# A decoder layer with soft experts: where the softmax weights are turned, and in which order the work ahead of the first expert is issued

## The chip, the cores and the metric

One core of a Trainium2 chip. The metric is the device time of one execution in microseconds (us): the median of 12 runs is 2963.4 us, from 2962.04 to 2964.12. Everything is fp32.

Engines go by their short names: PE is TensorE (PEld its weight loads), DVE is VectorE, ACT is ScalarE, POOL is GpSimd, SP is SyncE, which here only issues DMAs. Each runs its own instructions strictly in the order in which they were written, and waits on semaphores for the others.

## The reference, cut to what matters

32 sequences of 100 tokens, 256 features; 16 heads of 16; a context of 361 rows for each sequence; 8 experts with 128 slots each and a hidden layer of 1024.

```python
def _L0_attn_ref(x, Wq, Wk, Wv, Wo):            # self-attention, causal, rotary
    score = jnp.where(causal[None], jnp.einsum('bqd,bkd->bqk', q, k), -jnp.inf)
    attn = jax.nn.softmax(score / jnp.sqrt(jnp.float32(D_K)), axis=-1)
    out = jnp.einsum('bqk,bkd->bqd', attn, v)
...
def _L0_ffn_ref(x, norm_gamma, slot_norm_gamma, slot_embeds, w1, b1, w2, b2):
    logits = jnp.einsum('bnd,esd->bnes', xn, sn)
    dispatch = jax.nn.softmax(logits, axis=1)                     # over the 100 tokens
    combine = jax.nn.softmax(logits.reshape(b, n, e * s), axis=-1)
    slots = jnp.einsum('bnd,bnes->besd', xn, dispatch)
    h = jax.nn.gelu(jnp.einsum('besd,edh->besh', slots, w1) + b1[None, :, None, :], approximate=False)
    eo = jnp.einsum('besh,ehd->besd', h, w2) + b2[None, :, None, :]
    out = jnp.einsum('bmd,bnm->bnd', eo.reshape(b, e * s, DIM), combine)
x = x + _L0_attn_ref(_layernorm(x), ...)
x = x + _L0_xattn_ref(_layernorm(x), ctx_1024, ctx_1024, ...)     # cross-attention
x = x + _L0_ffn_ref(_layernorm(x), ...)
```

## The kernel before

The 32 sequences form 8 groups of 4 (SIZES, line 16). For each group the 8 experts run one after the other on all 4 sequences at once; so there are 64 turns of an expert, each with its weights loaded anew (load_first for w1, load_second for w2 and b2, lines 1212 to 1222). While the experts of one group run, the attention of the next group is worked in between their matmuls. The first group's attention has no experts to hide behind and runs ahead of them.

An expert's turn (run_expert, from line 1456) has two halves: 32 matmul instructions of 512 columns into ph, every four followed by a gelu on ACT (line 1479), then 64 instructions of 256 columns into pe (a matmul in the code is two instructions in fp32, a transpose one). After each half of pe a small product with the combine weights (py) is added to x. Before the turn, route (line 1376) makes what the expert needs. It subtracts the maximum (dT, line 1388), takes exponentials on ACT (line 1400), sums on DVE (line 1409), a reciprocal, and a product on POOL (line 1417): that is the dispatch softmax with slots on partitions and tokens along the row. The next matmul needs tokens on partitions, so four transposes on PE turn dT into pd, and DVE copies that to disp (line 1430). Then sl, 16 matmul instructions, gathers the slots, and DVE scales them into slT (line 1446). route also makes cT, the combine weights. It begins when 4 of the 32 matmuls of the pe half are done, for the next expert.

Self-attention of one sequence (self_attention, from line 862): scores, mask and maximum on DVE (lines 770, 780), a subtraction on POOL (line 787), exponentials on ACT (line 795), sums on DVE (line 800). self_turn (line 815) then turns the probabilities with 16 transposes on PE into ps_pT, four to a PSUM bank, and ACT copies each bank to pT (line 828). self_values multiplies with the values in 32 small matmul instructions (ps_av), each on a quarter of the array.

Cross-attention does not turn its probabilities on PE after the first group. VectorE's transpose turns each 32x32 square by itself (line 1063, tile xt), and two DMAs put the squares where they belong: one writes xt to a scratch tensor xd in DRAM (line 1075), one reads it back as xpT with rows and columns of squares exchanged (line 1082). The first group (early) uses PE and ps_xpT (cross_turn, line 1098).

The order of all instructions is set when the program is built, by a planner at the head of the file. It keeps a clock of its own (pe["t"], advanced by spend, line 258) and queues of jobs for the other engines. Each job has a duration and, for DMAs, a lag after which its data count as there. run (line 222) emits a job when the clock has come to the time at which its inputs should be ready; that fixes its place in its engine's queue. Pieces of attention are generators that yield a Need (what must be ready, how many PSUM banks); drive and between step them as soon as the planner thinks the need is met. On the chip an engine waits until its data are there, whatever the lag said. SP's queue is one such order: a read that waits for its write holds back all that stands behind it.

near (line 857) says how far ahead of the running group a stream may work. drive(routing, routing) after the preparation runs the first route alone. load_constants (line 459) issues the weights' loads on ACT's queue, 17 of them.

Of the kernel before, what the change touches and what calls it, by code (L numbers as in the profile page):

```python
# [14 lines left out]
P = 128  # L15
# [8 lines left out]
def decoder_layer(ctx: ExitStack, tc: tile.TileContext, a: dict, out: bass.AP):  # L24
# [28 lines left out]
    NXP = 3  # L53
# [28 lines left out]
    idle_from = {"DVE": 0.0, "ACT": 8.0, "POOL": 6.0, "SP": 0.0}  # L82
    tables = {"now": None, "gelus": 0}

    class Buf:
# [28 lines left out]
        def written(self, by):  # L114
            self.writes.append(by)
            if self.root is not None:
                self.root.writes.append(by)
            self.used(by)

# [165 lines left out]

    rings = {
# [12 lines left out]
    class Need:  # L299
# [3 lines left out]
        def __init__(self, *reads, banks=1, pairs=0, exps=None, when=None, t=0.0):  # L303
            self.reads, self.banks, self.pairs = reads, banks, pairs
            self.exps, self.when, self.t = exps, when, t

        def time(self):
            items = [w for b in self.reads for w in b.writes]
            if self.banks:
                items += rings["small"].due(self.banks)  # L310
            if self.pairs:
                items += rings["pairs"].due(self.pairs)
            t = ends(items)
            return None if t is None else max(t + HOP, self.t)
# [4 lines left out]
    class Steps:  # L319


        def __init__(self, it):
            self.it, self.need, self.result = it, Need(banks=0), None
# [11 lines left out]
        def step(self):  # L335
            reads = self.need.reads
            try:
                self.need = next(self.it)
            except StopIteration as end:
# [4 lines left out]
    def drive(goal, *streams):  # L344


        while goal.it:
            run()
            ready = [s for s in streams if s.fits()]
            if ready:  # L350
                ready[0].step()
# [34 lines left out]
    def ring(pool_, shape, name, bufs):  # L386
# [10 lines left out]
        "p": ring(one, [S, NH, S], "p", 1), "ropeu": ring(one, [P, 4 * S], "ropeu", 1),  # L397
# [6 lines left out]
        "pT": ring(two, [S, HG * S], "pT", NQ), "ctx": ring(two, [P, len(KC), D], "ctx", 2),  # L404
# [4 lines left out]
        "xd": ring(dram, [P, 4 * NKB * HG * QB], "xd", 3),  # L409
# [8 lines left out]
        "dT": ring(wk, [P, GM, S], "dT", 2), "cT": ring(wk, [P, NTM], "cT", 3),  # L418
        "disp": ring(wk, [S, GM * NS], "disp", 1), "slT": ring(wk, [P, ND, GM * NS], "slT", 1),
# [18 lines left out]
    def load_raw(nm, at):  # L438
        raw = R["hT"].new(f"raw{nm}")
        v = raw.get().rearrange("p (c d) -> p c d", c=ND)  # L440
        nc.scalar.dma_start(out=v, in_=a[f"L0_attn_{nm}"].rearrange("(c p) d -> p c d", p=P))
        raw.written(at)
        raws[nm] = raw

# [14 lines left out]
    def load_constants():  # L459

        load_raw("Wk", 5.5)
        load_raw("Wq", 8.0)
        nc.scalar.dma_start(out=rope, in_=a["rope"].rearrange("p (m f) n -> p m f n", f=2))
        load_raw("Wv", 11.0)
        load_raw("Wo", 12.5)
        rows = Buf(ap=one.tile([P, P], F32, name="rows"))
        for r0, src in (
# [6 lines left out]
            nc.scalar.dma_start(out=rows.ap[r0 : r0 + src.shape[0], :], in_=src)  # L474
        rows.written(14.0)
        for k, nm in enumerate(("Wk", "Wq", "Wv", "Wo")):
            w = wT["x" + nm] = fixed([P, ND, D], f"xw{nm}")
            nc.scalar.dma_start(
                out=w.ap, in_=a[f"L0_xattn_{nm}"].rearrange("(c p) o -> p c o", p=P)
            )  # L480
            w.written(15.5 + 1.5 * k)
        nc.scalar.dma_start(out=bvB, in_=a["L0_xattn_bv"].partition_broadcast(P))
        nc.scalar.dma_start(out=boB, in_=a["L0_xattn_bo"].partition_broadcast(P))
        se = Buf(ap=wpool.tile([P, NE, D], F32, tag="w1", name="se"))
        nc.scalar.dma_start(out=se.ap, in_=a["L0_ffn_slot_embeds"].rearrange("e s d -> s e d"))
        se.written(26.0)
        return rows, se

    def make_constants():
# [18 lines left out]
        gps(1.5, lambda: nc.gpsimd.memset(spad.ap, 0.0), [], [spad], prio=3)  # L508
        for i in range(2):
# [10 lines left out]
    def turn_rows(rows):  # L520
        ps = bank("ps_cols")
        transpose(ps.get()[:, :NROW], rows.ap[:NROW], ident[:NROW, :NROW])
# [224 lines left out]
    def self_scores(t, kT):  # L747
# [5 lines left out]
        sc = [rings["pairs"].new("sc") for _ in range(2)]  # L753
        for c in range(ND):
            for q in range(NQ):
                rows_ = slice(q * 32, (q + 1) * 32)
                matmul(
                    sc[q // 2].get()[:S, q % 2, c * 2 * S : (c + 1) * 2 * S],
                    lhsT=qT[rows_, c, :],
                    rhs=kT.get()[rows_, c, :, :],  # L760
                    share=NQ, start=True, stop=True,
                )
        parts = []
        for i in range(2):
            hs = slice(i * HPC, (i + 1) * HPC)
# [5 lines left out]
                    p.get()[:, hs, :].rearrange("n (q h) k -> n q h k", q=2),  # L771
# [9 lines left out]
                    nmax.get()[:, hs], p.get()[:, hs, :], axis=AX.X, op=ALU.max  # L781
# [6 lines left out]
                    p.get()[:, hs, :], p.get()[:, hs, :],  # L788
# [6 lines left out]
                lambda hs=hs: nc.scalar.activation(p.get()[:, hs, :], p.get()[:, hs, :], AF.Exp),  # L795
                [part], [part], table="exp",
            )
            vec(
                0.99,
                lambda hs=hs: nc.vector.tensor_reduce(  # L800
                    sums.get()[:, hs], p.get()[:, hs, :], axis=AX.X, op=ALU.add
# [11 lines left out]
        return p, parts, widened(rinv, NH, 0.29)  # L813

    def self_turn(p, parts):

        pTs = []
        for q in range(NQ):
            yield Need(parts[q // 2])
            ps = bank("ps_pT")  # L820
            for i in range(HG):
                transpose(
                    ps.get()[:S, i * S : (i + 1) * S], p.get()[:, q * HG + i, :], ident[:S, :S]
                )
            pT = R["pT"].new()
            act(
                0.49,
                lambda pT=pT, ps=ps: nc.scalar.copy(pT.get(), ps.get()[:S, : HG * S]), [ps], [pT],
# [877 lines left out]
```

## Time and profile before

| | |
|---|---|
| median of 12 runs | 2963.4 us |
| the profiled execution | 2963.39 us, of it the span from first to last instruction 2961.6 us |
| self-attention's transposes, ps_pT | 512 instructions, mean 249 ns |
| the copies to pT on ACT (line 828) | 128, mean 494 ns |
| dispatch's transposes, pd | 256 instructions, mean 273 ns |
| the copies to disp on DVE (line 1430) | 64, mean 688 ns |
| self-attention's values, ps_av | 1024 instructions of 100 columns |
| trips through DRAM, xd and xpT | 112 each way, 768 KB each |
| loads of expert weights, w | 128 of 1024 KB |
| bytes moved by DMA | 343.58 MB, mean 116 GB/s |
| first matmul of the first expert | 220.8 us after the span's start |

A mean duration of a matmul is the time from its start to its modelled end; matmuls overlap, so it is longer than the time that one takes away from the next. An engine's busy time is the union of these. A line "A <- B: total, times, longest" is idle time of A before the instructions named, and who ended it.

### The profile page before, as it was taken

How to read it: one execution, taken by the hardware profiler on the slowest of the kernel's cores; microseconds unless marked ns; L12 is line 12 of the kernel's file. 1: busy time of each engine (PE TensorE's matmuls, PEld its weight loads, DVE VectorE, ACT ScalarE, POOL GpSimd, SP SyncE). 2: the span in 40 equal slices, each digit the busy share in tenths (PEclk: the TensorE clock that was granted, in tenths of full speed). 3: DMA queues.
4: the chain of work that ended last, by engine and by line, in shares of the span. 5: the costliest groups of instructions: out<-in, count | busy, mean ns of one | idle time of the engine just before them, and what ended most of it. 6: DMA issues, size and time to landing. Idle time of an engine off the chain costs nothing.

```text
span 2961.6 us, 42941 instructions
## 1 busy us (share of the span) xinstructions
PE 2909.6 (98%) x17393; PEld 2033.2 (69%) x17393; DVE 1368.0 (46%) x2719; ACT 1234.3 (42%) x2662; POOL 555.1 (19%) x722
## 2 busy tenths in 40 slices
PE   6989999999999999999999999999999999999999
PEld 4766766767667676677667666677676766677676
DVE  5764554546443554436444355444554345422121
ACT  3554444444443444434444444433444434433331
POOL 3413231032101221013210222002321021000000
PEclk9989999999999999999999999999999999999999
DMA  3022433335352343414443343433344234422221
GB/s 111 12 70 69 167 103 121 133 116 170 109 178 68 130 148 125 157 58 151 132 156 119 98 151 126 147 111 119 123 156 141 92 105 162 167 72 70 73 75 52
DMA packets 191574, 343.58 MB, mean 116 GB/s; under 512 B 8104, under 2 KB 160656, under 8 KB 191376
## 3 DMA queue, kind: packets, MB, share of 16 engines
q1 hardware_dynamic: 187632, 337.18, 34.0%
q10 hardware_dynamic: 3744, 3.65, 0.4%
q8 instruction: 138, 2.26, 0.3%
q14 instruction: 60, 0.49, 0.1%
HBM read 249.44 MB, written 91.36 MB: 115 GB/s over the span
## 4 chain that ended last, share of the span: by engine, by line
PE 95%; ACT 2%; DVE 1%; POOL 1%; DMA 1%; issue 0%; SPq 0%; ACTq 0%; DVEq 0%; POOLq 0%
PE pe L268 31%; PE ph L268 30%; PE sc L268 5%; PE sl L268 4%; PE py L268 4%; PE ps_lt L268 3%; PE ps_xv L268 3%; PE ps_kT L268 3%; PE ps_xav L268 2%; PE ps_qk L268 2%; PE ps_o L268 2%; PE ps_pT L272 1%; PE pd L272 1%; PE ps_v L268 1%; PE sc L272 1%; PE ps_xq L268 1%
## 5 line engine op out<-in xcount | busy, mean ns | idle before, releaser
L268 PE MATMUL pe<-w,hT 128*128 128x256 f32 x4096 | 1000.8, 383 | 0.0
L268 PE MATMUL ph<-slT,w 128*128 128x512 f32 x2048 | 964.1, 599 | 1.5 <-ACT hT L1479 1.4
L268 PEld LDWEIGHTS pe<-w,hT 128*128 128x128 f32 x4096 | 742.2, 190 | 156.4 <-issue 52.7
L1479 ACT ACTIVATE hT<-ph,cols 128x512 f32<-128x512 f32 x512 | 350.5, 687 | 799.5 <-PE ph L268 799.3
L268 PEld LDWEIGHTS ph<-slT,w 128*128 128x128 f32 x2048 | 372.0, 190 | 325.2 <-issue 290.8
L1049 ACT ACTIVATE sc<-sc,xnmax 128x361 f32<-128x361 f32 x448 | 237.6, 530 | 146.1 <-DVE xnmax L1039 138.8
L1039 DVE TENSOR_REDUCE xnmax<-sc 128x2 f32<-128x722 f32 x256 | 222.0, 903 | 165.1 <-PE sc L268 164.7
L1063 DVE STREAM_TRANSPOSE xt<-sc 128x384 f32<-128x384 f32 x448 | 231.7, 556 | 23.5 <-ACT sc L1049 18.1
L608 POOL TENSOR_SCALAR ve<-bnmv 100x1 f32<-100x1 f32 x96 | 27.7, 289 | 907.7 <-DVE bnmv L605 907.6
L1417 POOL TENSOR_TENSOR dT<-dT,ri 128x400 f32<-128x400 f32 x64 | 54.6, 853 | 721.8 <-DVE ri L1414 720.6
L1531 DVE SCALAR_TENSOR_TENSOR x<-py,cinv,x 100x256 f32<-100x256 f32 x256 | 112.7, 477 | 153.2 <-PE py L268 153.0
L1409 DVE TENSOR_REDUCE sm<-dT 128x4 f32<-128x400 f32 x64 | 34.7, 542 | 263.9 <-ACT dT L1400 263.9
L787 POOL TENSOR_TENSOR p<-p,nmax 100x800 f32<-100x800 f32 x64 | 96.5, 1523 | 315.6 <-DVE nmax L780 312.6
L1508 DVE TENSOR_TENSOR eo<-pe,b 128x512 f32<-128x512 f32 x128 | 87.6, 684 | 129.2 <-PE pe L268 128.9
L268 PEld LDWEIGHTS sl<-disp,xn 100*128 100x128 f32 x1024 | 135.7, 194 | 8.1 <-issue 1.3
L268 PE MATMUL sl<-disp,xn 100*128 100x128 f32 x1024 | 136.7, 277 | 0.9 <-DVE disp L1430 0.9
L1446 DVE TENSOR_SCALAR slT<-sl,cols 128x512 f32<-128x512 f32 x128 | 95.4, 745 | 84.3 <-PE sl L268 83.6
L268 PE MATMUL py<-eo,cT 128*100 128x256 f32 x512 | 131.5, 379 | 0.8 <-DVE eo L1508 0.8
L268 PE MATMUL sc<-kT,xqT 32*128 32x361 f32 x1024 | 125.6, 518 | 3.7 <-DVE xt L1063 2.0
L770 DVE TENSOR_TENSOR p<-sc,causal 100x800 f32<-100x800 f32 x64 | 60.4, 985 | 137.8 <-PE sc L268 137.8
L428 ACT ACT_TABLE_LOAD x93 | 119.3, 1283 | 1.5
L268 PEld LDWEIGHTS py<-eo,cT 128*100 128x100 f32 x512 | 85.4, 167 | 50.1 <-issue 29.0
(144 smaller groups left out, 3231.1 us busy)
## 6 DMA issues: line engine op xcount, KB each, us to landing
w<-in_L_ffn_w_dram SPq DMA_DIRECT2D x128, 1024.0 KB
xd<-xt SPq DMA_DIRECT2D x112, 768.0 KB
xpT<-xd SPq DMA_DIRECT2D x112, 768.0 KB
ctx<-in_ctx_dram SPq DMA_DIRECT2D x32, 256.0 KB
b<-in_L_ffn_b_dram SPq DMA_DIRECT2D x64, 128.0 KB
ctx<-in_ctx_dram SPq DMA_DIRECT2D x32, 105.0 KB
x<-in_x_dram SPq DMA_DIRECT2D x8, 400.0 KB
out_dram<-x SPq DMA_DIRECT2D x16, 200.0 KB
```

The costliest lines, as they stand in the source:

```text
L268: nc.tensor.matmul(out, lhsT=lhsT, rhs=rhs, **kw)
L272: nc.tensor.transpose(out, in_, identity)
L428: act(0.2, lambda: nc.scalar.activation(spare, mhalf[:1, :1], f), [], [], table=table, prio=2)
L770: lambda i=i, hs=hs: nc.vector.tensor_tensor(p.get()[:, hs, :].rearrange("n (q h) k -> n q h k", q=2), sc[i].get()[:S, :, : HG * S].rearra ...
L787: lambda hs=hs: nc.gpsimd.tensor_tensor(p.get()[:, hs, :], p.get()[:, hs, :], nmax.get()[:, hs].unsqueeze(2).to_broadcast([S, HPC, S]), AL ...
L1039: lambda nm=nm, sc=sc: nc.vector.tensor_reduce(nm.get(), sc.get()[:, :, :SK], axis=AX.X, op=ALU.max, negate=True),
L1049: nc.scalar.activation(to[:, :SK], sc.get()[:, i, :SK], AF.Exp, bias=nm.get()[:, i : i + 1], accum_out=sums.get()[:, c, q, r : r + 1],)
L1063: nc.vector.transpose(t_.get()[:, :, :, 2 * t + i, :].rearrange("p j c u -> p c j u"), sc.get()[:, i, : NKB * P].rearrange("p (c u j) -> p ...
L1446: lambda dc=dc, sl=sl: nc.vector.tensor_scalar(slT.get()[:, dc, : nb * NS], sl.get()[:, : nb * NS], cols.ap[:, NGM + dc : NGM + dc + 1], N ...
L1479: lambda h=h, ph_=ph_, hc=hc: nc.scalar.activation(h.get()[:, :n], ph_.get()[:, :n], AF.Gelu, bias=cols.ap[:, e * NHC + hc : e * NHC + hc ...
L1508: lambda eo=eo, po=po, m=m: nc.vector.tensor_tensor(eo.get()[:, :m], po.get().rearrange("p (i d) -> p i d", i=2)[:, :m], b2.unsqueeze(1).t ...
L1531: lambda b=b, i=i: nc.vector.scalar_tensor_tensor(xs[g].get()[:, b, :], py[:S, i, :], k.ci.get()[:, b : b + 1], xs[g].get()[:, b, :], ALU. ...
```

## The change

Four things are changed. Dispatch weights: route is split in two. soften makes dT and disp for expert e + 1 while route for expert e only uses what lies ready. For the first expert of a group soften still turns on PE; for the others DVE turns squares into dt and there_and_back sends them through DRAM to disp. Self-attention: from the fifth sequence on, squares and there_and_back take the place of self_turn, in two halves of eight heads; the tiles p and dT are padded to 128 columns, with zeros set once by POOL. Planner: the allowance of each DMA falls from 5.0 us to 4.5 (cross) or 4.0 (the new ones), that of a pair of cross-attention's squares rises from 0.95 to 1.12 us; buffers are told free when their last reader is done; streams with a lower sequence number go first; xpT has two buffers instead of three, ctx one instead of two. Ahead of the first expert: three loads stay on ACT's queue, the rest go to SP's; the self-attention scores come half by half; near lets streams work further ahead; the first route is driven together with the streams.

```diff
-    NXP = 3
+    NXP = 2
-    idle_from = {"DVE": 0.0, "ACT": 8.0, "POOL": 6.0, "SP": 0.0}
+    idle_from = {"DVE": 0.0, "ACT": 3.0, "POOL": 5.0, "SP": 0.0}
...
             if ready:
-                ready[0].step()
+                min(ready, key=lambda s: s.need.seq).step()
...
-        "p": ring(one, [S, NH, S], "p", 1), "ropeu": ring(one, [P, 4 * S], "ropeu", 1),
+        "p": Kept([const.tile([P, NH, P], F32, name="p")]), "ropeu": ring(one, [P, 4 * S], "ropeu", 1),
...
-        "pT": ring(two, [S, HG * S], "pT", NQ), "ctx": ring(two, [P, len(KC), D], "ctx", 2),
+        "st": ring(two, [P, 4, HPC, QB], "st", 1),
+        "sd": ring(dram, [P, 4 * HPC * QB], "sd", 3),
+        "pT": ring(two, [P, 4, HPC, QB], "pT", 2), "ctx": ring(two, [P, len(KC), D], "ctx", 1),
...
-        "dT": ring(wk, [P, GM, S], "dT", 2), "cT": ring(wk, [P, NTM], "cT", 3),
-        "disp": ring(wk, [S, GM * NS], "disp", 1), "slT": ring(wk, [P, ND, GM * NS], "slT", 1),
+        "dT": Kept([const.tile([P, GM, P], F32, name=f"dT{i}") for i in range(2)]),
+        "dt": ring(wk, [P, 4, GM, QB], "dt", 1), "dd": ring(dram, [P, 4 * GM * QB], "dd", 2),
+        "cT": ring(wk, [P, NTM], "cT", 3),
+        "disp": ring(wk, [P, 4, GM, QB], "disp", 2), "slT": ring(wk, [P, ND, GM * NS], "slT", 1),
...
+    def load_cross(nm, at):
+        w = wT["x" + nm] = fixed([P, ND, D], f"xw{nm}")
+        nc.sync.dma_start(out=w.ap, in_=a[f"L0_xattn_{nm}"].rearrange("(c p) o -> p c o", p=P))
+        w.written(at)
...
+        load_raw(nc.scalar, "Wk", 5.0)
+        load_raw(nc.scalar, "Wq", 6.5)
         nc.scalar.dma_start(out=rope, in_=a["rope"].rearrange("p (m f) n -> p m f n", f=2))
+        load_raw(nc.sync, "Wv", 9.0)
+        load_cross("Wk", 10.0)
...
+        zeros = gps(3.0, lambda: nc.gpsimd.memset(R["p"].tiles[0], 0.0), [], [], prio=2)
+        R["p"].first.append(zeros)
+        for i in range(2):
+            zeros = gps(1.0, lambda i=i: nc.gpsimd.memset(R["dT"].tiles[i], 0.0), [], [], prio=3)
+            R["dT"].first.append(zeros)
...
+    def squares(p, part, hs):
+
+        st, sd, pT = R["st"].new(), R["sd"].new(), R["pT"].new()
+        vec(
+            1.2,
+            lambda: nc.vector.transpose(
+                st.get().rearrange("p j h u -> p h j u"),
+                p.get()[:, hs, :].rearrange("p h (u j) -> p h j u", j=4),
+            ),
+            [part], [st],
+        )
+        there_and_back(
+            st, st.get, sd, pT, lambda: pT.get().rearrange("p g h u -> p g (h u)"), 4.0
+        )
+        return pT
+
+    def there_and_back(t, source, d, to, target, lag):
+
+
+        job(
+            "SP", 0.35,
+            lambda: nc.sync.dma_start(
+                out=d.get(), in_=source().rearrange("p j h u -> p (j h u)")
+            ),
+            [t], [d], lag=lag,
+        )
+        job(
+            "SP", 0.35,
+            lambda: nc.sync.dma_start(
+                out=target(), in_=d.get().rearrange("(g u) (j f) -> (u j) g f", u=QB, j=4)
+            ),
+            [d], [to], lag=lag,
+        )
...
+        pairs_ = ((0,), (1,)) if state["group"] < 0 else ((0, 1),)
...
+            if not early:
+                pTs.append(squares(p, part, hs))
...
+                        to = av.get()[q * 32 : (q + 1) * 32, c * n : (c + 1) * n].rearrange(
+                            "p (g u) -> p g u", u=QB
+                        )
+                        pT = pTs[q // 2].get()[:S, :, (q % 2) * HG + h, :]
...
         last = FIRST[state["group"] + 1] + SIZES[state["group"] + 1]
-        return b < last + (ahead if state["group"] >= 0 else 1)
+        return b < last + ahead
...
-                    lambda: b in queries and b in keys and state["turned"] > n - NXP
-                    and (b >= SIZES[0] or state["flipped"] > n - 2)
+                    lambda: b in queries and b in keys
+                    and (state["flipped"] > n - 2 if b < SIZES[0] else state["turned"] > n - 4)
...
-    def route(k, e):
+    def soften(k, e, first=False):
...
+        disp = R["disp"].new()
+        if first:
+            yield Need(dT)
+            pd = bank("pd")
+            for b in range(nb):
+                transpose(pd.get()[:S, b * NS : (b + 1) * NS], dT.get()[:, b, :S], ident)
...
+        else:
+            dt = R["dt"].new()
+            vec(
+                0.7,
+                lambda: nc.vector.transpose(
+                    dt.get().rearrange("p j b u -> p b j u"),
+                    dT.get().rearrange("p b (u j) -> p b j u", j=4),
+                ),
+                [dT], [dt], prio=0,
+            )
+            there_and_back(
+                dt, dt.get, R["dd"].new(), disp,
+                lambda: disp.get().rearrange("p g b u -> p g (b u)"), 4.0,
+            )
+        k.disp[e] = disp
+
+    def route(k, e):
...
+        lt, disp = k.lt[e // 2], k.disp.pop(e)
...
                 matmul(
-                    sl.get()[:, b * NS : (b + 1) * NS],
+                    sl.get()[:, b * NS : (b + 1) * NS].rearrange("p (g u) -> p g u", u=QB),
                     lhsT=k.xn.get()[:, b, dc * P : (dc + 1) * P],
-                    rhs=disp.get()[:, b * NS : (b + 1) * NS],
+                    rhs=disp.get()[:S, :, b],
...
+    def routes(k, e):
+
+        if e == 0:
+            yield from soften(k, 0, True)
+        if e + 1 < NE:
+            yield from soften(k, e + 1)
+        return (yield from route(k, e))
+
+    routing = Steps(routes(groups[0], 0))
+    ready = drive(routing, routing, *order())
```

## The prediction

> **What bounds the kernel now.** I read the page's first two parts, then the windows table, then the chain of waits inside one expert, then who waits for whom. The page says which engine has no room:
>
> ```profile
> PE 2909.6 (98%) x17393; PEld 2033.2 (69%) x17393; DVE 1368.0 (46%) x2719; ACT 1234.3 (42%) x2662; POOL 555.1 (19%) x722
> ```
>
> PE is busy 2909.6 of 2961.6 us; 52.0 us are idle, and no other engine passes half. The windows table (window, its length, busy time of PE, PEld, DVE, ACT, POOL, granted clock, DMA share, GB/s) says where they lie:
>
> ```profile
> 0.00:20.00 20.00, 5.32 (x22) 4.29 (x23) 5.67 (x8) 2.33 (x4) 6.45 (x20) 1.00 0.76 217
> ...
> 200.00:220.00 20.00, 13.57 (x66) 12.01 (x66) 9.81 (x19) 7.41 (x13) 1.88 (x2) 0.76 0.42 137
> ...
> 400.00:800.00 400.00, 399.91 (x2575) 279.47 (x2574) 204.21 (x409) 173.99 (x381) 87.85 (x111) 1.00 0.39 130
> ```
>
> From 220 us, where the first expert begins, to 2400 us PE is idle for about 1.2 us. There a microsecond off PE's queue is a microsecond off the end, and work on any other engine is free until it makes PE wait. Before 220 us PE is idle for 42.9 us (20 minus its busy time, summed over eleven windows), and the granted clock drops: busy time times (1 - clock) gives 1.1 us at 40-60, 3.1 at 60-80, 1.4 at 180-200, 3.3 at 200-220 and 1.8 at 220-240, some 10.7 us of slowed work.
>
> **TensorE work removed and added.** A matmul row's mean (250 ns for a self-attention transpose) is its pipeline depth, not its cost; the cost is the step from one start to the next, which the chain of waits shows (start, length, what):
>
> ```profile
> 1001.84 0.88 PE ph L268 x2
> 1002.73 0.34 PE ps_pT L272 x4
> 1003.07 0.88 PE ph L268 x2
> 1003.96 0.69 PE ps_pT L272 x8
> ...
> 1008.65 0.82 PE ps_av L268 x32
> ...
> 1037.28 1.18 PE ps_xav L268 x48
> ...
> 1039.08 0.44 PE pd L272 x4
> ```
>
> Self-attention's turn: 16 transposes for each of the 28 sequences after the first group are gone, 448. Four take 0.34 and eight 0.69, so 0.0865 each: 38.8 us. The first group keeps its 64.
>
> Dispatch turn: 64 experts had four transposes at 0.44 us. The first expert of each of the 8 groups keeps them (first=True), 56 lose them: 24.6 us.
>
> Added: the 32 matmuls of ps_av run over 128 instead of 100 columns for those 28 sequences. With 48 at 1.18 and 32 at 0.82 (same columns), one is 0.0225 and 0.10 fixed; times 1.28 that is 0.0288, and 32 make 1.02. So 0.20 more, 5.6 us. Both new right-hand sides are read in four strided runs. ps_xav reads such runs already and is no dearer than ps_av, which reads contiguously (24.6 against 25.6 ns), so I add nothing for sl; if that failed for its 1024 matmuls, 10% of their 136.7 us would be 14 us.
>
> Net: 38.8 + 24.6 - 5.6 = **57.8 us off PE**.
>
> The Trainium skill speaks against this: VectorE: DVE Perf Modes, Rules for kernel authors, says to turn 128x128 on TensorE where PSUM will do, and its section The three transpose paths gives 390 ns for it and calls a plain strided DMA copy 19 times slower than the hardware's own DMA transpose when the inner stride is large. By 390 ns the 672 transposes would be worth 262 us, which the steps above contradict. The strided read of xpT, already in this trace with its long inner runs, shows no such slowness; the measurement decides.
>
> **Other engines.** ACT loses 112 copies at 494 ns (55 us). DVE gains 56 squares of 1024 columns and 56 of 512, and loses 56 copies at 688 ns. No such SBUF-to-SBUF square is in the trace; the nearest is
>
> ```profile
> L1063 DVE STREAM_TRANSPOSE xt<-sc 128x384 f32<-128x384 f32 x448 | 231.7, 556 | 23.5 <-ACT sc L1049 18.1 <-DMA xd<-xt 4.9
> ```
>
> 1.45 ns a column: at most 1.48 and 0.74 us; at least, at the rate of the 1024-column reduction (1224 ns), 1.22 and 0.61. I take 1.35 and 0.7: 76 + 39 - 39 = 76 us, so DVE goes from 46 to about 50%. Its tight place is an expert's second half, 18.60 of 24 us in a window of 1020-1044; two squares there make 21.3. It still fits. If it did not, PE would wait for eo, slT or the score banks.
>
> DMA: 112 trips there and back (56 self halves of 512 KB each way, 56 dispatch of 256 KB) add 86 MB to 343.58, and the share goes from 0.39 to about 0.48. On SP a read waits for its write, and everything behind it with it; the first line is SP's longest wait for DMA, the second is from PE's own list (total, times, longest):
>
> ```profile
> SPq L1082 <- DMA xd<-xt: 332.7, 99, 8.5
> ```
>
> ```profile
> PE ps_xav L268 <- DMA xpT<-xd: 2.3, 1, 2.3
> ```
>
> 3.36 us each for 768 KB, 8.5 at worst, yet PE waited for such a trip once. SP had 112 and gets 224, up to 4 for an expert of 43 us ((2961.6 - 220.8) / 64): 4 x 3.4 = 13 us of blocking. Queued behind it are w, ctx, b and x; w has an expert's half of slack (32 ph steps of 0.43, 14 us). The dispatch trip is made one expert (31.5 us from one ph to the next in the last group, more before) ahead, so it is hidden. The self and cross trips are used as soon as the planner thinks them landed, and it now allows 4.0 + 4.0 and 4.5 + 4.5 us where it allowed 5.0 + 5.0. Some will be late. From below 0 us; from above 2.3 us, the one late landing seen, for each of 28 sequences: 64 us. I take **5 us**, nearer the row: 1 wait in 112.
>
> **Ahead of the first expert.** ACT issues 17 loads in a row and waits in between for landings, so its first copies come late. First that stretch of the chain, then the one before the first expert:
>
> ```profile
> 13.22 3.08 DMA xwWq<-in_L_xattn_Wq_dram
> 16.30 1.27 ACT L938
> ```
>
> ```profile
> 213.78 0.86 POOL dT L1417
> 214.69 1.11 PE pd L272 x4
> 215.82 0.70 DVE disp L1430
> 216.65 3.75 PE sl L268 x16
> ```
>
> PE waits 6.4 us for xhT there (18.68 us). With three loads left on ACT, the copy can follow xh's transposes at 12.3, and PE starts ps_qk some **6 us** sooner. SP takes over fourteen issues, near 0.45 us each, and nothing computes on SP. POOL gets 2048 + 2 x 512 columns of memset; by vpad's row (1536 in 1.38) and xqT's (0.52 each) that is 2.9 us, up to which xh may be late. At the far end PE waits through chains such as the one shown: 180-220 has 10.95 us idle and 180-240 has 6.5 us of slowed work. The wider near() lets self-attention of sequences 5 and 6 begin early, some 5.7 us of PE each (ps_qk 1.76, ps_v, sc and ps_o 0.86 each, ps_av 1.02, small turns 0.4), and the first routing is now driven with the other streams; I take two thirds of 17.4, **12 us**. For 20-180 (17 us idle) I take nothing: the same two sequences put about 11 us of DVE work each (its rows summed, squares included) where DVE is already busy 17.64 of 20 (80-100 us). Together **18 us**; bounds from a loss of 5 (memsets and DVE late, nothing won) to a gain of 34 (6.4 + 17.4 + 10 of the middle).
>
> The clock: Trainium skill, TensorE: Matmul & The Clock Gate, Part 1, has an idle stretch of about 3.4 us halve the clock until work has run that long again. That fits 0.76 at 200-220, and by it filling the gaps there would win all of the 6.5, not two thirds.
>
> **Sum.** Span 2961.6 - 57.8 + 5 - 18 = 2890.8 us. The profiled run took 2963.4, 1.8 more than its span and the same as the median of the twelve, so **2892 us**.
>
> **Rivals.** (1) The new order wins nothing ahead of the first expert: the kernel loses 5 there, 2961.6 - 57.8 + 5 + 5 + 1.8 = 2916. For it: DVE at 88% in 80-100 us; against: the 6.4 us wait has one plain cause. (2) Landings come late at every self-attention: 64 us instead of 5 gives 2892 + 59 = 2951, most of the gain. For it: shorter allowances, twice the trips; against: one wait in 112 so far. (3) Slower: st has one buffer, so the second half's square on DVE waits for the first half's write, with everything behind it on DVE, and PE behind that. At 3.3 us for 28 sequences that is 92 us beyond the 5: 2984. It decides once more than 71 of the 92 reach PE. For it: the xt row above does wait for xd (4.9 us in all); against: the planner orders DVE's queue by those landings. That the new paths are not taken is open only for sequences 0-3 and each group's first expert, where the diff keeps the old ones; that is counted above.
>
> **How the numbers follow.** Forecast 0.68, rival 1 0.16, rival 2 0.08, rival 3 0.06; 0.02 for an end near no change. The likeliest one's own range is 2871 (a gain of 34 ahead of the experts, no stalls) to 2916. At the low end I add 168 blocks of transposes, each followed by a ph that takes 0.02 more (0.88 against 0.86): 3 us. At the high end I take in half of rival 2's stalls. That gives 2868 to 2925, where about 0.84 lies. A difference under 0.2% (6 us) can't be told from no change here: faster 0.92, same 0.02, slower 0.06.
>
> **What would show it.** ps_pT at 64 and pd at 32; ps_av about 1.02 us a sequence; STREAM_TRANSPOSE rows of 1024 and 512 columns at 1.2-1.5 and 0.6-0.75 us; the first ph at 208-215 us (what is won by moving work early shows later, as less of it between the experts); ps_qk starting near 13; PE waits on pT, xpT or disp landings of 5 us in total, none for disp. Wrong, if PE idles 20 us or more between 230 and 2800, by its waits for DMA (rival 2) or DVE's st waiting for sd (rival 3), or if the first ph comes after 220 (rival 1).

## The result, and the profile after

The changed kernel takes 2998.1 us (median of 7 runs, 2994.6 to 3000.4) against 2962.3 for the kernel before, a ratio of 1.0119 [1.0110, 1.0129]. It is slower; the forecast was 2892 us. The profiled execution has a span of 3000.2 us, 38.6 more than before.

The first line of the changed kernel's page:

```profile
PE 2893.2 (96%) x16721; PEld 2001.7 (67%) x16721; DVE 1485.3 (50%) x2775; ACT 1192.1 (40%) x2556; POOL 559.0 (19%) x725
```

PE has 672 instructions fewer (16721 against 17393), as forecast, but only 16.4 us less busy time, and it idles for 107.0 us instead of 52.0. The list of who made PE wait (engine, tile and line, what ended the wait; total, times, longest) says for what:

```profile
PE ps_av L280 <- DMA pT<-sd: 24.0, 9, 4.4
PE ps_xav L280 <- DMA xpT<-xd: 17.6, 11, 3.5
PE ph L280 <- DVE eo L1638: 12.8, 10, 1.8
```

Before, all late landings of xpT together cost 2.3 us. The windows table has the same columns as in the prediction, with the granted clock as the eighth entry:

```profile
0.00:20.00 20.00, 12.05 (x50) 9.90 (x51) 8.84 (x14) 3.65 (x6) 11.17 (x25) 1.00 0.74 208
...
200.00:220.00 20.00, 13.94 (x84) 11.38 (x84) 17.21 (x28) 7.94 (x22) 4.94 (x8) 0.86 0.44 159
220.00:240.00 20.00, 17.09 (x53) 9.22 (x52) 14.75 (x29) 11.08 (x27) 2.69 (x3) 0.54 0.26 93
400.00:800.00 400.00, 394.10 (x2459) 272.31 (x2458) 243.87 (x452) 175.23 (x396) 88.49 (x110) 0.99 0.53 181
```

In the first 20 us PE works 6.7 us more than before, the gain the prediction looked for there. Yet the first ph comes at 236.4 us instead of 220.8. Between 400 and 800 us, where PE had idled for 0.1 us, it now idles for 5.9 and the clock is no longer full.

Busy time is a poor ledger here, because a matmul at a lower clock is busy for longer. So I added up the steps of PE from one matmul's start to the next, and split each into its work at full clock, what a halved clock adds to it, and the idle part. This ledger runs from PE's first matmul to its last; some 10 us of the span lie outside it in each kernel, so its idle time is smaller than the 52.0 and 107.0 above. All in us:

| | first ph at | work | halved clock | idle |
|---|---|---|---|---|
| before | 220.8 | 2898.0 | 11.2 | 41.8 |
| after | 236.4 | 2842.1 | 50.7 | 97.0 |
| difference | +15.6 | -55.9 | +39.5 | +55.2 |

The differences sum to +38.8, the span's +38.6. Ahead of the first ph the work (168 us) and the idle time (36 to 37 us) are those of before, and the halved clock costs 26.5 us instead of 9.8. Behind it the idle time has gone from 4.6 to 60.8 us and the halved clock from 1.4 to 24.2.

One of the stalls, in the chain of waits (start, length, what):

```profile
1163.94 7.76 DMA sd<-st
1171.70 0.02 issue
1171.72 4.39 DMA pT<-sd
1176.11 0.04 issue
1176.15 1.09 PE ps_av L280 x28
1177.24 3.54 PE ph L280 x4
```

Write and read of one self-attention half take 12.2 us; the planner allows 4.0 + 4.0. PE waits for the landing, and then four ph steps take 3.54 us, twice the 1.74 they take elsewhere. What SP issued just before, and the granted clock in the windows around the stall:

```profile
1160.41 0.37 SPq L810 DMA_DIRECT2D xpT<-xd  x1
1161.65 0.37 SPq L810 DMA_DIRECT2D pT<-sd  x1
1162.41 0.37 SPq L1316 DMA_DIRECT2D w<-in_L_ffn_w_dram  x1
1162.83 1.02 SPq L1318 DMA_DIRECT2D b<-in_L_ffn_b_dram  x1
1163.94 0.70 SPq L803 DMA_DIRECT2D sd<-st  x1
1164.74 0.41 SPq L803 DMA_DIRECT2D xd<-xt  x1
1171.72 0.37 SPq L810 DMA_DIRECT2D pT<-sd  x1
```

```profile
1160.00:1171.00 11.00, 9.79 (x70) 5.49 (x71) 7.29 (x14) 4.59 (x8) 3.63 (x8) 1.00 0.96 321
1171.00:1176.00 5.00, 1.75 (x24) 0.57 (x14) 0.26 (x1) 0.00 (x0) 0.94 (x1) 1.00 0.80 249
1176.00:1181.00 5.00, 4.85 (x34) 2.60 (x35) 0.37 (x1) 0.69 (x1) 0.00 (x0) 0.66 0.41 147
1181.00:1190.00 9.00, 9.00 (x32) 4.58 (x32) 1.92 (x3) 4.34 (x7) 0.00 (x0) 1.00 0.13 23
```

Six transfers are issued within 4.4 us, a weight load of 1024 KB among them, and from 1160 to 1171 us the DMA engines are 96% busy at 321 GB/s. PE idles for 3.25 of the 5 us after that, and the clock drops to 0.66 in the 5 us that follow. A stall like this one, of 3.1 to 4.4 us at ps_av, stands once in six of the seven groups that still prepare another, with a stretch of 3.4 or 6.8 us at half clock behind it (521.7 to 528.5, 815.3 to 818.7, 1177.1 to 1180.5 for the first three).

### The profile page after: what moved, and what is told of

Same layout as the page of the kernel before. It is cut to its first block, busy times and chain, and to the rows that moved or that the text cites. A ratio compares the mean times of both kernels' runs of the same rounds, so it can differ in the third digit from the quotient of the medians.

```text
span 3000.2 us, 42116 instructions
## 1 busy us (share of the span) xinstructions
PE 2893.2 (96%) x16721; PEld 2001.7 (67%) x16721; DVE 1485.3 (50%) x2775; ACT 1192.1 (40%) x2556; POOL 559.0 (19%) x725
## 2 busy tenths in 40 slices
DMA packets 266836, 431.62 MB, mean 144 GB/s; under 512 B 11688, under 2 KB 221584, under 8 KB 266640
## 4 chain that ended last, share of the span: by engine, by line
PE 82%; DMA 9%; DVE 5%; ACT 1%; issue 1%; POOL 1%; SPq 0%; DVEq 0%; POOLq 0%; ACTq 0%
PE pe L280 26%; PE ph L280 26%; PE sc L280 4%; PE sl L280 4%; PE py L280 3%; DMA xpT<-xd 3%; PE ps_lt L280 3%; DMA sd<-st 3%; PE ps_xv L280 2%; PE ps_xav L280 2%; DMA xd<-xt 2%; PE ps_o L280 2%; PE ps_kT L280 2%; PE ps_qk L280 1%; DVE st L787 1%; DVE xt L1162 1%
## 5 line engine op out<-in xcount | busy, mean ns | idle before, releaser
L280 PE MATMUL ph<-slT,w 128*128 128x512 f32 x2048 | 979.7, 606 | 13.0 <-DVE eo L1638 12.8
L280 PE MATMUL pe<-w,hT 128*128 128x256 f32 x4096 | 986.1, 382 | 0.0
L280 PEld LDWEIGHTS pe<-w,hT 128*128 128x128 f32 x4096 | 752.3, 190 | 163.4 <-issue 56.3
L1148 ACT ACTIVATE sc<-sc,xnmax 128x361 f32<-128x361 f32 x448 | 238.0, 531 | 194.2 <-DVE xnmax L1138 186.9
L787 DVE STREAM_TRANSPOSE st<-p 128x1024 f32<-128x1024 f32 x56 | 113.6, 2029 | 1.2 <-DMA sd<-st 0.5
```

The costliest lines, as they stand in the source:

```text
L280: nc.tensor.matmul(out, lhsT=lhsT, rhs=rhs, **kw)
L787: lambda: nc.vector.transpose(st.get().rearrange("p j h u -> p h j u"), p.get()[:, hs, :].rearrange("p h (u j) -> p h j u", j=4),),
L1148: nc.scalar.activation(to[:, :SK], sc.get()[:, i, :SK], AF.Exp, bias=nm.get()[:, i : i + 1], accum_out=sums.get()[:, c, q, r : r + 1],)
```

## The experiments

The theory to test, A: the trips are late because the change cuts the planner's allowances for them while adding trips; each late one costs its wait and then a slower clock. Rivals: B, the planner's wrong duration of the squares on VectorE (the profile has 2.03 and 1.10 us where the plan says 1.2 and 0.7) misplaces what depends on them; C, the new order ahead of the first expert is what loses. Times are medians; ratios are to the kernel before. "Later idle" and "later clock" are PE's idle time and the cost of the halved clock behind the first ph, from the same ledger (after: 60.8 and 24.2 us).

**The planner's durations of the squares** (e1).

```diff
     def squares(p, part, hs):
         vec(
-            1.2,
+            2.05,
...
             dt = R["dt"].new()
             vec(
-                0.7,
+                1.1,
```

> Only two planner durations are changed to what the trace measured: a self-attention square 1.2 to 2.05 us, a dispatch square 0.7 to 1.1. Theory A (the planner's numbers for the new path are too short, so PE is put in front of data that are still on the way): PE's waits for eo and wide (12.8 + 4.5 us after 245 us) go, some of the 38.6 us of waits for pT and xpT too; idle of PE after 245 us from 57 to about 30, time 2998 to about 2955-2970. Theory B (twice the trips through SP and the DMA rings are simply too slow, whatever the plan says): waits for pT and xpT stay, time 2985-3000. Theory C (two xpT buffers and one ctx buffer instead of three and two are what is missing): as B.

Measured: 3053.9 us, 1.0309 [1.0293, 1.0324]; later idle 90.0, later clock 47.5. The list of PE's waits:

```profile
PE ps_xav L280 <- DMA xpT<-xd: 79.5, 33, 5.7
...
PE ps_av L280 <- DMA pT<-sd: 7.0, 2, 4.0
```

A truer duration makes the kernel 56 us slower: the self trips come in time, the cross trips do not. So B is not the cause. Why it is the cross trips that suffer was not traced further.

**The allowances** (e2 both, e3 both with e1's durations, e5 and e6 one each).

```diff
     def squares(p, part, hs):
...
-            st, st.get, sd, pT, lambda: pT.get().rearrange("p g h u -> p g (h u)"), 4.0
+            st, st.get, sd, pT, lambda: pT.get().rearrange("p g h u -> p g (h u)"), 8.0
...
-                    lambda: xpT.get().rearrange("p g c h u -> p g (c h u)"), 4.5,
+                    lambda: xpT.get().rearrange("p g c h u -> p g (c h u)"), 6.0,
```

> Only the planner's allowances for the trips are changed: self-attention 4.0 to 8.0 us each way, cross-attention 4.5 to 6.0; dispatch stays at 4.0. Theory A: PE's waits for pT and xpT (24.0 + 14.6 us after 245 us) fall under 5, the half-clock stretches after them go (47.6 us after 245 us, worth 23.8), time 2998 to about 2935-2950; the waits for eo and wide stay. Theory B: the later use only moves the waits, attention is late at the end of a group, time within 10 us of 2998. Theory C: xpT's two buffers are held longer, time 2998 or more.

> Durations and allowances of the two runs before together. Theory A: PE idle after 245 us under 10 (57 before), half clock there under 10 us, time 2998 - 54 - 20 = about 2920-2930. Theory B or C: no better than the better of the two alone, 2960 or more.

> Only the allowance of self-attention's trips is raised, 4.0 to 8.0 us; cross-attention stays at 4.5. e2 raised both and took 2912. If the late self trips (24.0 us of waits at ps_av, one of 3-4 us in each group behind a weight load) are the main cause, this run comes near e2: 2912-2935, ps_av waits near 0, ps_xav waits (14.6 us after 245 us) left. If the cut from 5.0 to 4.5 for cross-attention is the main cause, it stays above 2960.

> Only the allowance of cross-attention's trips is raised, 4.5 to 6.0 us; self-attention stays at 4.0. If cross trips are the main cause (e1, with true square times, had 79.5 us of waits at ps_xav and only 7.0 at ps_av), this run comes near e2: 2912-2945. If the self trips are, it saves some 20 us of 2998 and ps_av's 24 us of waits with their half-rate clock stay: 2965-2985.

| | self, cross allowance | time | ratio | later idle | later clock |
|---|---|---|---|---|---|
| after | 4.0, 4.5 | 2998.1 | 1.0119 [1.0110, 1.0129] | 60.8 | 24.2 |
| e2 | 8.0, 6.0 | 2911.8 | 0.9834 [0.9819, 0.9848] | 2.6 | 0.3 |
| e3 | 8.0, 6.0, durations of e1 | 2925.2 | 0.9880 [0.9864, 0.9897] | 12.4 | 2.6 |
| e5 | 8.0, 4.5 | 2948.1 | 0.9951 [0.9936, 0.9966] | 29.6 | 6.6 |
| e6 | 4.0, 6.0 | 2956.3 | 0.9975 [0.9964, 0.9987] | 30.2 | 15.4 |

Two numbers in the plan are worth 86 us (2998.1 - 2911.8); PE, DVE and POOL run as many instructions as in after (ACT 12 fewer). PE's whole waiting list for DMA from 240 us on, in e2:

```profile
PE ps_xav L280 <- DMA xpT<-xd: 1.1, 2, 0.6
```

The waits for eo and wide that stood in the list of after are gone as well, though nothing was done about them: they followed from the late trips. The two allowances about add up (alone they win 50 and 42 us, together 86). Each leaves the other's waits, first e5, then e6:

```profile
PE ps_xav L280 <- DMA xpT<-xd: 20.1, 14, 3.6
```

```profile
PE ps_av L280 <- DMA pT<-sd: 27.0, 9, 5.2
```

The slower clock falls with the idle time: some 0.1 to 0.5 us on top of each microsecond of stall. A holds: longer allowances alone remove the waits. It leaves open how much of the need for them comes from the shortened allowances and how much from the added trips, as no run gives the changed kernel the 5.0 us a way of before.

**The look-ahead and the first routing** (e4 on the changed kernel, e10 on the best version, below).

```diff
-        return b < last + ahead
+        return b < last + (ahead if state["group"] >= 0 else 1)
...
-    ready = drive(routing, routing, *order())
+    ready = drive(routing, routing)
```

> Only the two edits that put more work ahead of the first expert are undone: near() as before while no group runs, and the first routing driven alone. The loads' order, the half-by-half scores and the squares stay. Theory A says the 15.6 us by which the first ph is later (236.4 against 220.8) are slowed clock (53.9 us at half rate before it against 22.4) and work done early, caused by these two: first ph at 212-222 us, but 11 us of self-attention come back later, so time 2998 to about 2985-2995. A rival: the load order or the half scores do it; then the first ph stays at 230 us or more and the time at 2998.

Measured: 3007.7 us, 1.0155 [1.0140, 1.0170]; the first ph at 235.9 us (after 236.4). The late first expert does not come from these two edits, and the rest of the order was still open. The time is 9.6 us above that of the changed kernel, with intervals that lie apart: here the two edits do win something (PE's idle time ahead of the first ph is 42.5 us without them, 36.1 with them).

**Scores in one piece ahead of the first expert** (e7, with the allowances of e2).

```diff
-        pairs_ = ((0,), (1,)) if state["group"] < 0 else ((0, 1),)
+        pairs_ = ((0, 1),)
```

> e2 with one more edit undone: self-attention's scores ahead of the first expert are issued in one piece for both halves again, not half by half. In the result PE waited 13.1 us at sc ahead of the first expert (4.3 before) and ran 53 us at half rate there (19.7 before). If the halves cause that, first ph comes at 220-228 us (238.0 in e2) and the time falls to about 2898-2906. If the loads' order, the streams' order or the two xpT buffers do, first ph stays at 233-240 and the time at 2905-2918.

Measured: 2902.5 us, 0.9799 [0.9784, 0.9814], the fastest of all with e10; first ph at 226.0 us instead of 238.0 in e2, 9.3 us less time on the machine; later idle 1.6, later clock 0.0. Its first line, and the windows at the end of the first stretch and between the experts:

```profile
PE 2854.8 (99%) x16721; PEld 1982.8 (68%) x16721; DVE 1485.0 (51%) x2775; ACT 1190.7 (41%) x2544; POOL 556.3 (19%) x725
```

```profile
200.00:220.00 20.00, 13.72 (x48) 7.99 (x48) 17.10 (x34) 10.69 (x28) 4.23 (x4) 0.55 0.48 163
220.00:240.00 20.00, 20.00 (x150) 13.18 (x145) 8.75 (x20) 8.89 (x19) 3.62 (x5) 0.86 0.58 198
400.00:800.00 400.00, 399.87 (x2416) 276.19 (x2414) 230.98 (x427) 171.97 (x372) 83.24 (x108) 1.00 0.52 177
```

The DMA share between the experts is 0.52, as high as in the changed kernel, and PE idles for 0.1 us. So the traffic by itself does not cost PE time when the plan leaves room for it.

**Dispatch turned on PE again** (e8, with the allowances of e2).

```diff
-            yield from soften(k, e + 1)
+            yield from soften(k, e + 1, True)
```

> e2 with the dispatch weights turned by PE's transposes for every expert, still one expert ahead; self-attention keeps its squares. It prices the dispatch part of the change. By the steps of pd in the trace (0.44 us for 56 experts) the time rises by 24.6: 2912 to about 2937. If freeing SP and DVE of 56 trips and squares is worth something, less: 2925-2935. If the trips were harmful, below 2912.

Measured: 2949.1 us, 0.9957 [0.9942, 0.9972], 37.3 us above e2. Of it 24.7 are PE's work, the forecast's 24.6; later idle and clock add 11.3 (11.4 + 2.8 against 2.6 + 0.3). The dispatch part is worth its price at the least.

**The rest of the order ahead of the first expert**, undone on e7: the order of streams (e9), the look-ahead (e10, diff above), the loads' queue (e12), and all of these (e13).

```diff
-                min(ready, key=lambda s: s.need.seq).step()
+                ready[0].step()
...
-    idle_from = {"DVE": 0.0, "ACT": 3.0, "POOL": 5.0, "SP": 0.0}
+    idle_from = {"DVE": 0.0, "ACT": 8.0, "POOL": 5.0, "SP": 0.0}
...
-        load_raw(nc.sync, "Wv", 9.0)
+        load_raw(nc.scalar, "Wv", 9.0)
...
```

> e7 (both allowances raised, whole scores: 2902.5, first ph 226.0) with the streams taken in their fixed order again instead of the lowest sequence first. If the order by sequence helps ahead of the first expert, first ph is later than 226 and the time above 2906; if it is one of the causes of the slow stretch, first ph comes at 218-223 and the time at 2893-2899; otherwise within 3 us of 2902.5.

> e7 with the look-ahead of near() and the filled first routing undone. My forecast took 12 us of gain from these two. If that holds, the time rises to 2910-2915. If e4 is right, where undoing them in the result moved the time by 3 us or more upwards with first ph unchanged, 2902-2912. If they are what keeps 201.8-225.7 us at half rate, first ph falls under 220 and the time under 2899.

> e7 with the weights' loads issued on ACT's queue again, in the new order. It prices the 6 us that my forecast took for freeing ACT. If that holds, PE's first ps_qk starts near 18 us instead of 13, first ph is 4-6 us later (230-232) and the time 2906-2909. A rival: the early start is paid back before the first expert (in the result idle ahead of it was 36.1 us against 37.2), then within 2 us of 2902.5.

> The whole scores and long allowances of the best version so far (2902.5 us), and all four edits to the order ahead of the first expert undone together: the loads back on ACT's queue, the first stream that fits instead of the one set earliest, the old look-ahead of one sequence, the first routing alone. What is left of the change is then almost only the squares. If the order is worth something that single undoings hid, because one edit covers for another, this run is 10 us or more above the best version (2912 to 2925). If the order as a whole wins nothing, it is within 6 us (2897 to 2909), and the 18 us of the forecast are empty. By the sum of the single undoings (4.8 + 4.3 - 0.6) it is 2911.

| | undone on e7 | time | ratio | first ph at | idle ahead of it |
|---|---|---|---|---|---|
| e7 | nothing | 2902.5 | 0.9799 [0.9784, 0.9814] | 226.0 | 31.9 |
| e9 | order of streams | 2907.3 | 0.9821 [0.9806, 0.9836] | 236.6 | 37.5 |
| e10 | look-ahead, first routing | 2901.9 | 0.9797 [0.9782, 0.9812] | 210.0 | 32.2 |
| e12 | loads on ACT's queue | 2906.8 | 0.9820 [0.9804, 0.9836] | 232.7 | 37.9 |
| e13 | all three | 2911.9 | 0.9827 [0.9813, 0.9842] | 234.6 | 45.2 |

The last two columns are of one profiled execution each. Beside the long allowances the look-ahead and the filled first routing win nothing: without them the first ph comes 16 us earlier, but 9.6 us less work has been done by then, and neither the idle time ahead of it nor the end moves. The intervals of e9 and e12 overlap with e7's, so their 4.8 and 4.3 us are not clear of the noise. All of them together are worth 9.3 us by the medians, though the intervals of e7 and e13 just touch. That is near the sum of the single undoings (8.5).

e13 also shows that something else loses time ahead of the first expert. The four edits to the order there are undone in it, and the scores are whole, and still its first ph comes 13.8 us later than in the kernel before (220.8), with 8.0 us more idle time (45.2 against 37.2). PE waits 10.8 us for the cross-attention squares there (2.0 before):

```profile
PE sc L284 <- DVE xt L1162: 5.5, 1, 5.5
PE sc L280 <- DVE xt L1162: 5.3, 2, 3.6
```

Of the change there remain, among others, the fewer buffers for xpT and ctx, the zeros, the split routing and the squares of the fifth and later sequences. Which of these does it was not tested.

**Squares that read neighbouring columns** (e11).

```diff
-                p.get()[:, hs, :].rearrange("p h (u j) -> p h j u", j=4),
+                p.get()[:, hs, :].rearrange("p h (j u) -> p h j u", j=4),
...
-                    dT.get().rearrange("p b (u j) -> p b j u", j=4),
+                    dT.get().rearrange("p b (j u) -> p b j u", j=4),
```

> e7 in which DVE's new squares read their 32x32 blocks from neighbouring columns instead of every fourth column; so keys and tokens are put at the wrong places and the output is not the reference's. It asks why a square of 1024 columns takes 2.03 us (1.98 ns a column) and one of 512 takes 1.10, while xt takes 1.44 ns a column out of PSUM. If the step of four in the read is the cause, the two fall to about 1.1 and 0.6 us; if it is SBUF as the source or the shape of the writes, they stay at 2.0 and 1.1.

Measured: 2901.4 us in one run, so no difference from e7. The groups of instructions (busy time, mean ns of one), first of e7, then of e11:

```profile
L787 DVE STREAM_TRANSPOSE st<-p 128x1024 f32<-128x1024 f32 x56 | 113.1, 2019 | 27.6 <-DMA sd<-st 27.5
L1532 DVE STREAM_TRANSPOSE dt<-dT 128x512 f32<-128x512 f32 x56 | 61.7, 1102 | 7.6 <-POOL dT L1508 7.6
```

```profile
L787 DVE STREAM_TRANSPOSE st<-p 128x1024 f32<-128x1024 f32 x56 | 68.6, 1225 | 26.3 <-DMA sd<-st 26.2
L1532 DVE STREAM_TRANSPOSE dt<-dT 128x512 f32<-128x512 f32 x56 | 39.3, 701 | 7.6 <-POOL dT L1508 7.6
```

Reading every fourth column costs 0.8 us of 2.0 and 0.4 of 1.1. VectorE has room for it.

**The weights over another queue** (e14, on the changed kernel with its short allowances): is a trip late because it stands behind the load in SP's queue, or because both share the DMA engines?

```diff
-        nc.sync.dma_start(out=w1, in_=a["L0_ffn_w1"][e].rearrange("(c p) h -> p c h", p=P))
+        nc.scalar.dma_start(out=w1, in_=a["L0_ffn_w1"][e].rearrange("(c p) h -> p c h", p=P))
...
-        nc.sync.dma_start(out=w2, in_=a["L0_ffn_w2"][e].rearrange("(c p) d -> p c d", p=P))
+        nc.scalar.dma_start(out=w2, in_=a["L0_ffn_w2"][e].rearrange("(c p) d -> p c d", p=P))
```

> The changed kernel with its own short allowances, but w1 and w2 of every expert are loaded over ACT's queue instead of SP's; the trips stay on SP's. If a trip is late because it stands behind a 1 MB load in SP's own queue, the 7.7 us from write to read fall to some 3.5 us, the waits of ps_av for pT and of ps_xav for xpT (41.6 us) fall below 15 us, the slowed clock with them, and the time to about 2940. If the load and the trip share the DMA engines and their bandwidth whichever queue they are issued from, the gap stays above 6 us where a load has just been issued, the waits stay above 30 us and the time near 2998.

Measured: 3004.9 us, 1.0146 [1.0129, 1.0163]. PE's waits, and the same place in the chain, one group on:

```profile
PE ps_av L280 <- DMA pT<-sd: 24.1, 7, 4.8
...
PE ps_xav L280 <- DMA xpT<-xd: 11.2, 11, 2.3
```

```profile
1537.18 8.06 DMA sd<-st
1545.25 4.50 DMA pT<-sd
1549.79 1.35 PE ps_av L280 x28
1551.14 3.27 PE ph L280 x4
```

The load was issued by ACT at 1535.86, and the write still takes 8.06 us, with the DMA engines 99% busy at 317 GB/s from 1537 to 1545. Over the whole run a sd write that SP waited for, with a weight load issued within 4 us of it, takes 7.8 us in the median (7.6 in the changed kernel), and the others 3.8 (3.1), also in the median. Single ones of the others reach 7.8 (8.7). So it is not the place behind the load in SP's queue. With the DMA engines 96 to 99% busy, their shared bandwidth is the explanation that is left, though the other trips do still stand on SP's queue.

## Why the prediction was wrong, step by step

**The step that failed: "I take 5 us, nearer the row: 1 wait in 112".** The row was read from a plan with allowances of 5.0 + 5.0 us. The change moves exactly that: at 4.0 + 4.0 and 4.5 + 4.5 the waits for pT and xpT are 41.6 us, the waits that follow from them make it 56.2 us more idle time behind the first ph than before, and the allowances of e2 take nearly all of it away. One wait in 112 said that 10 us was enough for the traffic of before, not that 8 or 9 would be for twice as many trips; the half shown above took 12.2. What the trace of before did hold was the spread: a read that SP held back for its xd write went out 3.3 us after the write in the median of 79 cases, but with a weight load close by up to 8.9, as the quoted "8.5 at worst" says. PE meets the worst case once or so in each group.

**Its price was wrong too.** Rival 2 is what happened in kind, with 20 late landings (9 of pT, 11 of xpT) and not one at every self-attention; the test set for it (20 us of idle between 230 and 2800) came out. But its 64 us had no term for the clock. The stalls behind the first ph cost 56.2 us of idle and 22.8 of slowed work, more than the upper bound. The prediction had quoted the page TensorE: Matmul & The Clock Gate, Part 1, of the Trainium skill, and used it only for what lies ahead of the first expert. The trace agrees with its window of some 3.4 us: behind the first ph the slow stretches are one or two times 3.4 us long, as in the clock of 0.66 from 1176 to 1181 shown above. It does not bear out that an idle stretch must last that long: a wait of 3.1 us was followed by one, and so were pairs of waits of 1.1 to 1.8 us.

**"Together 18 us" ahead of the first expert** failed as well: after loses 15.6 us there, and rival 1's sign (a first ph after 220) came true too. Term by term: the 6 us from ACT freed of loads appear where they were forecast. ps_qk starts at 11.9 us instead of 18.7, with 6.7 us more PE work in the first 20 us. Undoing that part brings ps_qk back to 18.1 us and 6.0 us more idle time, though the 4.3 us of time are not clear of the noise (e12). The 12 us from filling the gaps with the look-ahead come out as 9.6 on the changed kernel (e4) and as nothing beside the long allowances (e10). Scores half by half, a part of the change the sum did not price, lose 9.3 us (e2 against e7), and e13 leaves a further loss there that the sum did not price either. Why even e7, with less idle time than before ahead of its first ph (31.9 us against 37.2), has 19.6 us of halved clock there against 9.8 stays open. Part of it may be chance: e11, in the same order but with quicker squares, had 28.4 us of it at 27.7 us of idle time. So the bound "from a loss of 5" was too near.

**PE's work, "57.8 us off PE"**, came close: 55.9 in after, 63.2 in e7, where PE hardly stalls behind the first ph. From 245 us on ps_pT fell by 38.0 us (38.8 forecast) and pd by 24.6 (24.6). ps_pT is at 64 and pd at 32 instructions. The steps of ps_av sum to 26.3 us for 26 sequences in e2, 1.01 each (1.02 forecast). The strided reads cost sl next to nothing (113.4 us against 112.8 for 1008 matmuls). Three figures of the prediction don't follow from its own words, without weight for the outcome: its sum gives 2892.6 us, not 2892; half of rival 2's 59 us more on rival 1's 2916 is 2945, not 2925; and its 86 MB of trips are 86016 KB, 88 MB in the units of the 343.58 (431.62 in after).

**The squares' cost** was outside the bounds: 2.03 and 1.10 us against at most 1.48 and 0.74. The upper bound came from xt, which reads PSUM; its strided read costs 1.44 ns a column, the strided read of SBUF 1.97, and a dense one 1.20 (e11). It made no difference to the end: DVE went to 50%, as forecast.

**Rival 3** was not it. st waits for sd only 0.5 us in after. In e7 it waits 27.5 us and PE still idles for 1.6 us behind the first ph: the wait exists, but PE does not need what is queued behind it. **The trips of dispatch** are hidden as forecast; no wait of PE for disp's landing stands in the list.

The idea of the change was worth what its PE work says: e7 and e10 are 60 us faster than the kernel before, nearly all of it PE's work (63.2 us; idle and slowed work sum to 53.0 before and 53.1 in e7). Both beat the two kernels.

## What to carry to other kernels

When a change shortens an allowance that a plan is built on, or adds traffic to it, the waits seen under the old one say little of the new one: look at the slowest trips in the trace, those that meet a big load, and compare the allowance with them. Where PE sets the end, an allowance that was too long by several microseconds cost nothing that could be seen here, and one that was too short cost the wait plus up to half as much again by the clock. Price a stall on TensorE with the work at half clock behind it.

## What the runs showed of the hardware that was not expected

- A transfer beside a large load is as slow when the load is issued by another engine: with 317 to 321 GB/s moving, a 512 KB write takes 8 us whether the 1024 KB load beside it was issued by SP or by ACT (3 to 4 us in the median of the writes without a load close by).
- Behind the first ph of the changed kernel each of the seven waits of 3.1 to 4.4 us is followed by 3.4 or 6.8 us of half clock, the single waits of 2.7 and 3.0 us by none; three more such stretches follow two waits of 1.1 to 1.8 us close together. Over the whole kernel the halved clock costs 50.7 us, against 11.2 before, at 97.0 and 41.8 us of idle time. The sum of the idle time does not give its price: ahead of the first ph the idle time hardly differs (36.1 and 37.2 us), and the halved clock costs 26.5 and 9.8.
- VectorE's transpose of 32x32 squares, 1024 columns fp32 from SBUF to SBUF, takes 1225 ns when it reads neighbouring columns and 2019 when it reads every fourth; 512 columns take 701 and 1102.
